# A graph layer's edge sums: the second half of each unit is summed first, and the first half is matched against 13 destinations instead of the second against 18

## The chip, the cores and the metric

The kernel runs on one core of one Trainium2 chip, as one launch. The metric is device microseconds of one execution, from the first to the last work of that core; lower is better. The five engines are named as the profile names them: PE (TensorE), DVE (VectorE), ACT (ScalarE), POOL (GpSimd) and SP (SyncE).

## The reference

The kernel computes one relational graph layer behind a layer norm, with N = 12,500 nodes, E = 212,500 edges, 256 features in and out and R = 8 edge types:

```python
src = concatenate([_s, _d, arange(12500)])     # 100,000 random pairs both ways, and a loop at every node
dst = concatenate([_d, _s, arange(12500)])
order = argsort(dst, stable=True)              # edges sorted by destination, a node's loop last
edge_type_8 = randint(0, 8, (212500,))

h = maximum(layernorm(x), 0)
hx = einsum('ni,rio->rno', h, weight)
agg = segment_sum(hx[edge_type, src], dst)
out = x + agg * 0.5**0.5 + h_bias + (h @ loop_weight) * 0.5**0.5
```

There are 17 edges to a destination on average (212,500 / 12,500), its own loop among them, and they come sorted by destination.

## The kernel before

**Sums first, weights after.** The kernel does not build `hx`. It sums the source rows of `h` for each pair of destination and type, and multiplies the sums by the eight weight matrices afterwards. `acc` in SBUF is a ring of 768 destinations by 8 types, transposed, in two chunks of 128 features (`KC` = 2).

**Units and tiles.** Edges are cut into units, and one unit fills at most two tiles of 128 edges (`PAIR` = 2). The first 128 units (block 0) have exactly 256 edges. Every later unit takes `EDGES` = 267 consecutive edges; the last edges of up to 22 destinations in it (the loops) are taken out and handled elsewhere (`last_edges`), and the others are moved together (`compacted`), so that the rest fits in 256 places. The very last unit takes what remains: 212,500 − 128·256 − 673·267 = 41 edges. So there are 802 units and, since the last has one tile only, 1,603 tiles. Blocks are groups of 128 units whose indices are prepared together, one unit per partition.

**A unit's window.** `bases` gives each unit a base destination: the destination of its first edge, held between bounds (`low`, `high`) that are worked out from the unit's number. Both bounds are themselves held between 0 and N − `WIN` = 12,478, so that a window of `WIN` = 22 destinations never leaves the graph. `columns` turns an edge into a column number (destination − base)·8 + type + 1, with 0 for an edge that falls outside of what its half is matched against. `REACH` gives that for each half as (first destination, number of destinations): in the kernel before, the first half of a unit reaches over destinations 0 to 21 of the window and the second over 4 to 21.

```python
def to():
    for h, _, n in halves:
        nc.vector.scalar_tensor_tensor(
            got["there"][:, h], got["col"][:, h], float(n * R), got["there"][:, h],
            op0=ALU.is_le, op1=ALU.mult)
```

`final`, `valid`, `sum_` and `all_` then set the columns outside to 0, count per unit the edges with a column above 0, add the loops that were taken out, and leave the number in `counts`.

**The check at the end, and the second way through.** When the last block is prepared, `verdict` adds all `counts` and compares the total with E:

```python
nc.vector.tensor_scalar(flag, pt[0:1, 0:1], float(E), None, op0=ALU.not_equal)
...
with tc.If(state["general"]):
    general_path(tc, x, src, dst, etype, bias, out, h32, w, wl, ident)
```

All engines load `flag` (`load`, L629) and branch on it at the end of the program (L1243), when all the work above is done. `general_path` computes the layer again for any edges at all, and it overwrites `out`. It is two loops at run time. `nodes` (97 rounds of 128 nodes and one of 84) loads 128 rows of `h32` and `x`, transposes the former, multiplies by the loop weights and then by each of the 8 weight matrices with one PSUM tile between PE and DVE, and stores 128 KB to `acc` and 1 MB to `hx` in DRAM. `edges` (1,660 rounds of 128 edges and one of 20) loads 128 sources, destinations and types one to a partition and the destinations once more as a 128x128 tile; compares them on DVE; gathers 128 rows of `hx` with an indirect DMA on POOL; multiplies by the 128x128 matrix of equal destinations on PE; copies the sums out on DVE; and adds them to `acc` with a second indirect DMA on POOL that accumulates in DRAM. Its pools have one buffer each, and between two rounds all engines meet. Last, `acc` is copied to `out`.

**The main loop.** For each tile, in an order written out by hand: `gather(t + 58)` issues the tile's 128 source rows as an indirect DMA on POOL (L755) into one of 60 buffers; every 48th tile is fetched row by row from SP instead (L767), with source numbers that `kept_sources` keeps. `onehots` compares four tiles' columns with a row of 1 to 176 on DVE (L785), which gives one-hots of 176 columns. `edge_sums` (L818) multiplies the gathered rows, as the stationary operand, with the one-hots: per tile two matmuls, one for each chunk of features, and each shows as two records in the trace. The first tile of a unit starts the PSUM bank and writes all 176 columns; the second adds its 18·8 = 144 columns from column 32 on. `add_sums` (L832) adds the bank to the ring on DVE. When a group of 128 destinations is complete, `product` (L1009) multiplies its sums by the weights, in pieces that are queued between the tiles. The gathers of the first 96 tiles read `x` and are normalised on ACT (L713), since `h32` isn't written yet.

Of the kernel before, what the change touches and what calls it, by code (L numbers as in the profile page):

```python
# [14 lines left out]
ALU = mybir.AluOpType  # L15
# [7 lines left out]
P = 128  # L23
# [9 lines left out]


WIN = 22
REACH = ((0, 22), (4, 18))

GROUP = 128

# [5 lines left out]
AHEAD = 58  # L45

SINGLE = 48
# [7 lines left out]
PAIR = 2  # L55
# [164 lines left out]
def kernel(  # L220
# [11 lines left out]
    nc = tc.nc  # L232
    N, D = x.shape
    E = src.shape[0]
    R = weight.shape[0]
    KC = D // P
    C = R * max(n for _, n in REACH)
    assert KC * R * WIN <= 512
    plan = Plan(N, E)

    NT = plan.NT
    U = PAIR * P
# [32 lines left out]

    def place_of(t):
        u, i = divmod(t, PAIR)
        return u // P, i, u % P


    with ExitStack() as main:
# [29 lines left out]
        msg, oh, offsets, kind = {}, {}, {}, {}  # L311
        firsts, stops, loops, marked, typed, gidx, col = {}, {}, {}, {}, {}, {}, {}
        added, zeroed = {}, {}
        single, fetches = {}, []
# [42 lines left out]
        def kept_sources(b, got):  # L357

            def keep():
                single[b] = idx.tile([P, P], I32, name="single")  # L360
                nc.vector.tensor_single_scalar(
                    single[b], got["sf"][:, P:U], float(D * 4), op=ALU.mult)

            return [keep]

# [115 lines left out]
        def columns(b, got):  # L481


            halves = [(slice(i * P, (i + 1) * P), o, n) for i, (o, n) in enumerate(REACH)]

# [18 lines left out]
                        got["there"][:, h], got["col"][:, h], float(o), None, op0=ALU.is_ge)  # L504

            def plain_to():
                nc.vector.scalar_tensor_tensor(
                    got["there"][:, :U], got["col"][:, :U], float(WIN), got["there"][:, :U],
                    op0=ALU.is_lt, op1=ALU.mult)

            def plain_typed():
                nc.vector.scalar_tensor_tensor(
# [67 lines left out]
            if b == 0:  # L580
                return [
                    bases, plain, plain_from, plain_to, plain_typed, plain_final, plain_sum, *turned(
                        got, "col", lambda: col.setdefault(b, cols.tile([P, U], F32, name="cols")))]
# [155 lines left out]
        def gather(t):  # L739
            if t % PAIR == 0:  # L740
                both = msgs.tile([P, PAIR, D], F32, name="msg")
                for i in range(PAIR):
                    msg[t + i] = both[:, i, :]
            if t % QUAD:
                kind[t] = kind[t - 1]
            else:
                kind[t] = "h" if state["h32"] is not None and t >= state["h32"] + LATE else "x"
            table = {"h": h32, "x": x}[kind[t]]
            b, i, u = place_of(t)
            if b and i and kind[t] == "h" and t % SINGLE == SINGLE - 1 and t + AHEAD < NT:  # L750
                for r in range(0, P, SOURCES):
                    fetches.append((done["tile"] + HOLD, lambda r=r: load_sources(t, r)))
                return
            at = i * P + u
            nc.gpsimd.indirect_dma_start(  # L755
                out=msg[t], out_offset=None, in_=table[:, :],
                in_offset=bass.IndirectOffsetOnAxis(ap=gidx[b][:, at : at + 1], axis=0))

        def load_sources(t, r0):

            b, _, u = place_of(t)
            _, vals = nc.values_load_multi_w_load_instructions(  # L762
                single[b][u : u + 1, r0 : r0 + SOURCES], engines=[SP],
                min_val=0, max_val=(N - 1) * D * 4,
                skip_runtime_bounds_check_because="clamped to the table where they are computed")
            for i, v in reversed(list(enumerate(vals))):
                fetches.insert(0, (0, lambda i=i, v=v: nc.sync.dma_start(  # L767
                    msg[t][r0 + i : r0 + i + 1, :].bitcast(U8),
                    h32_bytes[:, bass.ds(v, D * 4)])))
# [6 lines left out]
        def onehots(t):  # L776

            n = min(QUAD, NT - t)
            o = ohs.tile([P, QUAD // PAIR, PAIR, C], F32, tag="oh", name="oh")
            b, _, u = place_of(t)  # L780
            k = 0
            for v, i in ((n // PAIR, PAIR), (1, n % PAIR)):
                if v and i:
                    of = col[b].rearrange("p (i u) -> p u i", i=PAIR)[:, u + k : u + k + v, :i]
                    j = nc.vector.tensor_tensor(  # L785
                        o[:, k : k + v, :i, :],
                        iota_f.unsqueeze(1).unsqueeze(1).to_broadcast([P, v, i, C]),
                        of.unsqueeze(3).to_broadcast([P, v, i, C]), op=ALU.is_equal)
                    k += v
            for i in range(n):  # L790
                oh[t + i] = o[:, i // PAIR, i % PAIR, :]
                made[t + i] = j.ins.name

        def load_offsets(u0):
# [8 lines left out]
        def edge_sums(t):  # L803
            m, o = msg.pop(t), oh.pop(t)
            if t % PAIR == 0:
                bank = banks[t // PAIR % BANKS]
                sums["ps"] = bank[:, : KC * R * WIN].rearrange("p (c k) -> p c k", c=KC)
            ps = sums["ps"]
            i = t % PAIR
            from_, width = (a * R for a in REACH[i])  # L810
            end = t == NT - 1 or i == PAIR - 1
            free = added.get(t // PAIR - BANKS)
            if i == 0 and free is not None and latest["pe"] is not None:
                tc.add_manual_dep(latest["pe"], free.name, SYNC_DEP, reason="bank is free")
            if i == 0 and latest["pe"] is not None:
                tc.add_manual_dep(latest["pe"], made[t], SYNC_DEP, reason="one-hots are made")
            for c in range(KC):
                j = nc.tensor.matmul(  # L818
                    ps[:, c, from_ : from_ + width], m[:, c * P : (c + 1) * P], o[:, :width],
                    start=(i == 0 and c == 0), stop=(end and c == KC - 1))  # L820
            latest["pe"] = j.ins
            return ps
# [126 lines left out]
        got = {}  # L949
# [104 lines left out]
        with tc.manual_schedule():  # L1054
# [21 lines left out]
            for t in range(min(AHEAD, NT)):  # L1076
                gather(t)
# [76 lines left out]
            for t in range(0, min(NT, LEAD + 1), QUAD):  # L1154
                onehots(t)
            for t in range(NT):
                done["tile"] = t
                if t + AHEAD < NT:
                    gather(t + AHEAD)
# [22 lines left out]
                if t % QUAD == 2 and t + LEAD + QUAD - 2 < NT:  # L1182
                    onehots(t + LEAD + QUAD - 2)
                    credit -= 0.89
                if t % (PAIR * REGS) == 0 and t // PAIR + REGS < NU:
                    load_offsets(t // PAIR + REGS)
                ps = edge_sums(t)
                while late and late[0][0] <= t:
                    late.pop(0)[1]()
# [18 lines left out]
                while queue and (budget > 0 and t >= queue[0][0] or t >= queue[0][1]):  # L1208
                    _, _, c, f = queue.pop(0)
# [4 lines left out]
                while waiting and (len(waiting) > LAG or t == NT - 1):  # L1214
                    u, ps = waiting.pop(0)
# [54 lines left out]
```

## Time and profile before

| | |
|---|---|
| median of 3 runs | 2020.3 us (2017.76 to 2020.92) |
| profiled execution: its own time | 2023.05 us |
| its span from first to last instruction | 2021.3 us |
| mean granted TensorE clock | 0.957 |
| PE busy | 1796.2 us (89%) |
| POOL busy | 1500.7 us (74%) |
| DVE busy | 1317.4 us (65%) |
| ACT busy | 218.4 us (11%) |

The busy times are of one profiled execution. The share of POOL counts an indirect DMA's instruction (951 ns on average) and not the time between two of them. PE's time is a sum over pipelined matmuls, so a busy PE may still have room. Where rows carry a "q" behind the engine's name (SPq, POOLq, DVEq), they are of the engine's sequencer: DMA issues, semaphores, branches.

### The profile page before, as it was taken

The numbers are of one execution on the slowest core, as the hardware profiler recorded it, in microseconds if no ns is written. First come the engines' busy times: TensorE is split into PE (matmuls) and PEld (weight loads), VectorE is DVE, ScalarE is ACT, GpSimd is POOL, SyncE is SP. The second block draws the span as 40 slices with busy tenths as digits, with TensorE's granted clock in tenths as the row PEclk, the third lists the DMA queues.
The fourth block names the chain that finished last, engine by engine and source line by source line (L and its number), as shares of the span: only waits on it lengthen the run. The fifth ranks groups of instructions, "written<-read, shape, count | busy, mean of one in ns | idle before, by whom it ended". The sixth has DMA issues, their size and how long they took to land.

```text
span 2021.3 us, 36386 instructions
## 1 busy us (share of the span) xinstructions
PE 1796.2 (89%) x10411; PEld 1610.0 (80%) x10411; DVE 1317.4 (65%) x3281; ACT 218.4 (11%) x470; POOL 1500.7 (74%) x1602
## 2 busy tenths in 40 slices
PE   2468999997999898999899999998998898998998
PEld 2357999997888888988788788787787787787886
DVE  7869566687656578656577655577665568665642
ACT  7854110000000000000000000000000000000000
POOL 7766777777777777777777777777777777777773
PEclk8569999998999999999999999999999999999999
DMA  8973443444444444444444444444444444444442
GB/s 296 380 222 97 146 138 106 128 138 127 129 139 118 139 137 117 130 118 139 130 126 139 128 124 135 132 122 140 129 118 138 125 123 129 118 138 123 118 120 73
DMA packets 152577, 281.63 MB, mean 139 GB/s; under 512 B 31149, under 2 KB 101940, under 8 KB 152372
## 3 DMA queue, kind: packets, MB, share of 16 engines
q0 software_dynamic: 75648, 206.67, 35.1%
q1 hardware_dynamic: 76724, 72.61, 11.4%
q8 instruction: 82, 1.34, 0.3%
q14 instruction: 123, 1.01, 0.2%
HBM read 253.55 MB, written 25.60 MB: 138 GB/s over the span
## 4 chain that ended last, share of the span: by engine, by line
PE 38%; DMA 20%; SPq 17%; issue 12%; POOL 7%; DVE 5%; ACT 2%; DVEq 0%; POOLq 0%; ACTq 0%
PE ps L818 20%; PE po L1009 17%; DMA msg<-h,gidx 13%; SPq L767 13%; POOL msg L755 7%; SPq L762 4%; DMA hr<-h 2%; DMA h<-xt 1%; DVE e_stats L701 1%; DVE acc L832 1%; ACT xt L713 1%; DMA xr<-in_x_dram 1%; DMA w<-in_L_gnn_weight_dram 1%; DMA msg<-h 1%; DVE oh L785 1%
## 5 line engine op out<-in xcount | busy, mean ns | idle before, releaser
L755 POOL DMA_INDIRECT msg<-h,gidx x1480 | 1407.7, 951 | 464.2 <-issue 371.1
L818 PE MATMUL ps<-oh,msg 128*128 128x176 f32 (+1 forms) x6412 | 1169.6, 312 | 201.5 <-DMA msg<-h,gidx 78.5
L818 PEld LDWEIGHTS ps<-oh,msg 128*128 128x128 f32 x6412 | 1037.8, 196 | 355.3 <-DMA msg<-h,gidx 159.1
L1009 PE MATMUL po<-w,acc 128*128 128x256 f32 x3136 | 883.0, 383 | 1.8 <-DVE acc L832 1.8
L832 DVE TENSOR_TENSOR acc<-acc,ps 128x352 f32 x802 | 415.1, 518 | 503.4 <-PE ps L818 499.1
L1009 PEld LDWEIGHTS po<-w,acc 128*128 128x128 f32 x3136 | 537.6, 192 | 25.3 <-DVE acc L832 2.6
L785 DVE TENSOR_TENSOR oh<-fixed,cols 128x704 f32<-128x704 f32 x402 | 353.0, 879 | 0.0
L881 DVE SCALAR_TENSOR_TENSOR acc<-types,pt 128x256 f32<-128x256 bf16 (+1 forms) x688 | 249.0, 411 | 77.5 <-PE pt L859 71.5
L864 ACT ACTIVATE self_t<-pt 128x256 f32<-128x256 f32 x98 | 37.5, 383 | 1456.4 <-DVE acc L881 1352.5
L755 POOL DMA_INDIRECT msg<-in_x_dram,gidx x96 | 91.0, 948 | 31.1 <-issue 24.4
L1009 PE MATMUL po<-wl,self_t 128*128 128x256 f32 x392 | 105.2, 391 | 4.9 <-ACT self_t L864 2.5
L1009 PEld LDWEIGHTS po<-wl,self_t 128*128 128x128 f32 x392 | 69.1, 196 | 11.4 <-ACT self_t L864 2.9
L1021 DVE TENSOR_TENSOR xr<-xr,po 128x256 f32<-128x256 f32 x98 | 40.5, 413 | 17.5 <-PE po L1009 15.7
L713 ACT ACTIVATE xt<-xt,n_shift,n_rstd 128x256 f32<-128x256 f32 x98 | 50.9, 588 | 8.6 <-DVE n_shift L710 8.6
L713 ACT ACTIVATE msg<-msg,e_shift,e_rstd 128x256 f32<-128x256 f32 x96 | 49.6, 589 | 12.8 <-DVE e_shift L710 12.8
L1022 DVE TENSOR_TENSOR xr<-xr,po 128x256 f32<-128x256 f32 x98 | 41.2, 420 | 3.4
L934 ACT ACTIVATE diagonal<-ident,kinds 128x128 bf16<-128x128 f32 x88 | 28.1, 390 | 135.0 <-DVE kinds L931 130.1
L859 PE MATMUL pt<-ident,hr 128*128 128x128 f32 x196 | 37.9, 275 | 0.0
L370 DVE TENSOR_SCALAR moves<-fixed 128x267 int32<-128x267 int32 x84 | 36.0, 428 | 1.1
L701 DVE BATCH_NORM_STATS2 n_stats<-xt 128x6 f32<-128x256 f32 x98 | 34.4, 412 | 2.5 <-DMA xt<-in_x_dram 1.7
L371 DVE COPY_PREDICATED fixed<-moves,fixed 128x266 int32<-128x266 int32 (+6 forms) x84 | 33.7, 401 | 2.9
L701 DVE BATCH_NORM_STATS2 e_stats<-msg 128x6 f32<-128x256 f32 x96 | 33.5, 411 | 0.0
(201 smaller groups left out, 319.7 us busy)
## 6 DMA issues: line engine op xcount, KB each, us to landing
msg<-h SPq DMA_DIRECT2D x3456, 1.0 KB
msg<-h,gidx POOLq DMA_INDIRECT x1480
xt<-in_x_dram SPq DMA_DIRECT2D x24, 512.0 KB
h<-xt SPq DMA_DIRECT2D x24, 512.0 KB
xr<-in_x_dram SPq DMA_DIRECT2D x24, 512.0 KB
hr<-h SPq DMA_DIRECT2D x24, 512.0 KB
out_dram<-xr SPq DMA_DIRECT2D x24, 512.0 KB
w<-in_L_gnn_weight_dram SPq DMA_DIRECT2D x2, 1024.0 KB
```

The source lines that it names most:

```text
L701: nc.vector.bn_stats(stats[:n, j, :], rows_[j])
L713: nc.scalar.activation(rows_[j], rows_[j], AF.Relu, bias=shift[:n, j : j + 1], scale=rstd[:n, j : j + 1])
L755: nc.gpsimd.indirect_dma_start(out=msg[t], out_offset=None, in_=table[:, :], in_offset=bass.IndirectOffsetOnAxis(ap=gidx[b][:, at : at + 1 ...
L762: _, vals = nc.values_load_multi_w_load_instructions(single[b][u : u + 1, r0 : r0 + SOURCES], engines=[SP], min_val=0, max_val=(N - 1) * D ...
L767: fetches.insert(0, (0, lambda i=i, v=v: nc.sync.dma_start(msg[t][r0 + i : r0 + i + 1, :].bitcast(U8), h32_bytes[:, bass.ds(v, D * 4)])))
L785: j = nc.vector.tensor_tensor(o[:, k : k + v, :i, :], iota_f.unsqueeze(1).unsqueeze(1).to_broadcast([P, v, i, C]), of.unsqueeze(3).to_broa ...
L818: j = nc.tensor.matmul(ps[:, c, from_ : from_ + width], m[:, c * P : (c + 1) * P], o[:, :width], start=(i == 0 and c == 0), stop=(end and ...
L832: i = nc.vector.tensor_tensor(a, a, ps, op=ALU.add)
L881: i = nc.vector.scalar_tensor_tensor(acc[:, :, r, s0 : s0 + n], of, float(r + 1), pst[:, :, :n], op0=ALU.is_equal, op1=ALU.mult)
L1009: i = nc.tensor.matmul(got["out", g][:n], lhs, rhs, start=(r == R and c == 0), stop=(r == R - 1 and c == KC - 1))
L1021: nc.vector.tensor_add(rows_[:n, k, :], rows_[:n, k, :], outs[g % 2][:n, 1, :])
L1022: nc.vector.tensor_add(rows_[:n, k, :], rows_[:n, k, :], got["out", g][:n])
```

## The change

The two tiles of a unit change places in the order of the sums. `place_of(t)` gives a unit's even tile the second half of its edges and its odd tile the first half; the last unit, which has one tile, keeps its first half. The even tile starts the bank and writes 176 columns as before. The odd tile, now the first half, adds 13·8 = 104 columns from column 0 on. `REACH` is (0, 13) for the first half and (0, 22) for the second, and `columns` uses these numbers for all units. `kept_sources` keeps the first half's sources, as the tiles that SP fetches are odd. In block 0, `plain_to` becomes one instruction per half. The number and the order of all other instructions are the same; behind `plain_to` the lines of the kernel after stand two further down (L755 becomes L757, L818 becomes L820).

```diff
-REACH = ((0, 22), (4, 18))
+REACH = ((0, 13), (0, 22))
...
     def place_of(t):
         u, i = divmod(t, PAIR)
-        return u // P, i, u % P
+        half = 0 if PAIR * u + 1 == NT else PAIR - 1 - i
+        return u // P, half, u % P
...
                 single[b] = idx.tile([P, P], I32, name="single")
                 nc.vector.tensor_single_scalar(
-                    single[b], got["sf"][:, P:U], float(D * 4), op=ALU.mult)
+                    single[b], got["sf"][:, :P], float(D * 4), op=ALU.mult)
...
             def plain_to():
-                nc.vector.scalar_tensor_tensor(
-                    got["there"][:, :U], got["col"][:, :U], float(WIN), got["there"][:, :U],
-                    op0=ALU.is_lt, op1=ALU.mult)
+                for h, o, n in halves:
+                    nc.vector.scalar_tensor_tensor(
+                        got["there"][:, h], got["col"][:, h], float(o + n), got["there"][:, h],
+                        op0=ALU.is_lt, op1=ALU.mult)
...
-            if b and i and kind[t] == "h" and t % SINGLE == SINGLE - 1 and t + AHEAD < NT:
+            if b and t % PAIR and kind[t] == "h" and t % SINGLE == SINGLE - 1 and t + AHEAD < NT:
...
-                oh[t + i] = o[:, i // PAIR, i % PAIR, :]
+                oh[t + i] = o[:, i // PAIR, place_of(t + i)[1], :]
...
-            from_, width = (a * R for a in REACH[i])
+            width = R * (REACH[0][1] if i else WIN)
...
-                    ps[:, c, from_ : from_ + width], m[:, c * P : (c + 1) * P], o[:, :width],
+                    ps[:, c, :width], m[:, c * P : (c + 1) * P], o[:, :width],
```

## The prediction

> **What bounds the kernel now.** I read the page's groups first, then POOL's own instructions in order of time, the matmuls by shape, and the chain.
>
> ```profile
> L755 POOL DMA_INDIRECT msg<-h,gidx x1480 | 1407.7, 951 | 464.2 <-issue 371.1
> ```
>
> ```profile
> 127.55 0.95 POOL L755 DMA_INDIRECT msg<-h,gidx  x1 [0.30 <-issue]
> ...
> 133.88 0.94 POOL L755 DMA_INDIRECT msg<-h,gidx  x1 [4.14 <-ACT e_rstd L705]
> ...
> 140.96 0.95 POOL L755 DMA_INDIRECT msg<-h,gidx  x1 [4.89 <-issue]
> ...
> 1994.17 0.95 POOL L755 DMA_INDIRECT msg<-h,gidx  x1 [0.30 <-issue]
> 1995.42 1.17 POOL L755 DMA_INDIRECT msg<-h,gidx  x1 [0.30 <-issue]
> ```
>
> The second fence is POOL in order of time. A gather takes 0.95 us and the next comes 0.30 us later, 1.25 us in all, from 4.75 us to 1995.4 us. 1,575 steps of 1.25 us are 1,970 of these 1,991 us. The only longer gaps are six between 128 and 196 us, 14.7 us in sum. So the stream of gathers is the bound, not PE with its 89%.
>
> ```profile
> L818 PE MATMUL ps<-oh,msg 128*128 128x176 f32 x3208 | 645.8, 325 | 69.8 <-DMA msg<-h,gidx 37.4 <-ACT msg L713 29.5
> L818 PE MATMUL ps<-oh,msg 128*128 128x144 f32 x3204 | 562.2, 298 | 131.7 <-DMA msg<-h 45.5 <-DVE acc L832 43.7 <-DMA msg<-h,gidx 41.1
> ```
>
> In the matmuls by shape, PE itself waits for messages. A narrower matmul lets it wait longer.
>
> **What the change does as written.** Half of the matmuls go from 144 to 104 columns. In the chain below, four records of 176 columns take 0.60 us and four of 144 take 0.49, so 32 columns are worth 27 ns a record and 40 columns 34 ns: 3,204 records × 34 ns = 110 us of PE time. If the time to load 128 weight columns sets a floor, the nearest row is the transposes of 128 columns, 0.11 us apart, against 0.1225: 3,204 × 12 ns = 40 us. Either is off the bound. POOL issues as many gathers at the same pitch. The six early gaps are the only place where PE's pace could help, as POOL waits there for buffers that PE frees; but PE itself waited 10.1 us for ACT's normalising at 120 to 131 us. I bound this gain by 0 and 13 us (14.7 less six ordinary pitches' 0.30) and take 2. The other edits cost nothing that ends last: one more DVE instruction in block 0 (0.3 us at most, behind gathers that run anyway), the swapped halves (as many rows, the same 1 KB), the SP-fetched tiles (still odd, their sources from the half that is now odd). If only this counted, the time would be some 2,018 us.
>
> **The step that I think decides: the last unit.** `columns` takes 13 destinations for the first half of every unit. The last unit's base isn't its first destination: `high` holds it at 12,500 − 22 = 12,478. Its 41 edges belong, at 17 to a destination, to the last two or three nodes; I worked the reference's inputs through, and its first destination is 12,498, so its columns stand at destinations 20 and 21 of the window. Before, 22 reach them. Now `to` asks for a column of at most 13·8 = 104, and theirs are 161 and up: 39 edges (41 less two loops) are set to 0 and not counted. `edge_sums` does give this tile 176 columns, but the numbers are gone by then. In the other 801 units both halves fit. The total is 212,461, not 212,500, `flag` is 1, and all engines take the branch into `general_path`. It comes after everything else, so it is added whole.
>
> ```profile
> L629 DVEq TENSOR_LOAD <-flag x1: 311/311/311, 1772.6 to 1772.6; - x1
> ```
>
> ```profile
> L1243 POOLq INC_SWDGE_SEM  x1: 2016/2016/2016, 1993.3 to 1993.3; - x1
> ...
> L1243 DVEq COMPARE_BRANCH  x1: 72/72/72, 2016.9 to 2016.9; - x1
> ```
>
> The flag is read at 1773 us and DVE branches at 2017 us; nothing of the second way runs in the trace before, so its rounds are priced by near rows.
>
> ```profile
> 0.82 2.06 DMA nat_s<-in_src_dram
> ...
> 113.42 13.67 DMA w<-in_L_gnn_weight_dram
> ...
> 1979.16 2.73 DMA msg<-h,gidx
> 1984.17 4.06 DMA msg<-h,gidx
> ```
>
> ```profile
> 1994.16 0.49 PE ps L818 x4
> ...
> 1995.09 0.60 PE ps L818 x4
> ```
>
> ```profile
> L1266 SPq EVENT_SEMAPHORE  x14: 17/28/28, 2019.7 to 2021.3; - x14
> ...
> L1266 SPq DRAIN  x3: 7/7/13, 2020.5 to 2020.8; - x3
> ```
>
> The first of these is the chain of the whole run (start, duration), the second the chain near its end, the third the program's end.
>
> **A round of `edges`** is a string of waits, with one buffer each:
> - Loads: SP issues the third load 0.93 us after the first (0.82 and 1.75 us in its queue), and such a load lands 2.06 us later: 3.0 us. Columns of 4 bytes have no row; I allow 2.6 to 4.0.
> - DVE makes the row numbers from the third load: 0.14 and 0.16 us (128x1 rows) and a hand-over of 0.15: 0.45. Its other comparisons lie under the gather.
> - Gather: 2.73 to 4.1 us from POOL's start to landing; 2.8, since nothing else uses the queue.
> - PE, two records of 256 columns: 0.6 us at full clock, 1.2 at half (the profile grants 0.50 at 50 to 100 us, where PE is half idle); 1.0.
> - DVE copies the sums: 0.42 and two hand-overs: 0.6.
> - The accumulating scatter: no row. At least a gather's 2.75, and twice that, 5.5, if it reads and then writes; 4.0, between the two, since the fixed part needn't be paid twice.
> - The meeting of all engines: the program's end takes 0.8 us from SP's first drain to the last semaphore; twelve more semaphores are 0.3 us, the branch 0.07 to 0.23, and `INC_SWDGE_SEM` 0.03 us at the start of the program but 2.0 at its end. 1.2 to 3.3; I take 3.0, as its gathers are as fresh as at the end.
>
> Sum 14.85 us, between 10.95 and 19.2. Times 1,661: **24.7 ms**, between 18.2 and 31.8.
>
> The Trainium skill (DMA: Bandwidth & Descriptors, Anatomy of one DMA) puts one DMA at 2.0 us and bytes / 436 GB/s, 2.3 us for these 128 KB. The trace's gathers are dearer, 2.73 us at best. By the page's figure for gather and scatter the round would be 12.6 us by my estimate and the whole time 26.4 ms.
>
> **A round of `nodes`**: loads 2.5 (0.45 more than one), transposes 0.55, copy 0.6, loop weights 1.0 (four records of 256, 1.03 in PE's order of time); then eight times four records, a copy and two hand-overs (1.03 + 0.42 + 0.3 = 1.75, 14 in all; 22 at half clock), 16; the 1 MB store, 10 (the 1 MB of weights took 13.7 in a crowded stretch, 512 KB of `hr` 4.5 to 6.9); the meeting 3.0. Sum 33.7, between 29 and 45. Times 98: 3.3 ms, between 2.8 and 4.4. The last copy moves 12.8 MB both ways: 25.6 MB at the 380 GB/s of the busiest slice are 67 us, at the mean 139 GB/s 184; 0.1 ms.
>
> **Sum.** The profiled execution's own time is 2,023 us (span 2,021), 2.8 us above the median of the three runs, which doesn't matter here. 2.02 + 24.67 + 3.30 + 0.10 = **30.1 ms**. Ends: 23.1 and 38.4 ms.
>
> **Rivals.**
> - The second way is not taken (0.04). I would have to have misread the count; against that, the same reckoning of the kernel before gives 212,500 exactly. Then the stream of gathers decides, as above: 2,018 us, from 2,007 (all of the early gaps) to 2,023. Hence 0.01 for faster by more than 0.2% (about what a measurement of this kernel can tell from no change) and 0.03 for within 0.2%.
> - A dear round (0.10): the round costs 6 us more than my sum, in the accumulating scatter or in the branch back. From 20.9 us a round on, the whole is over 40 ms. For it speaks that neither has a row, and that the crowded queue's loads at 118 to 126 us took 2.1 to 2.8 us to issue alone; against it that the queue is empty here. The Trainium skill (Runtime: NRT & Kernel Launch, Instruction fetch mechanics) says that a taken branch to a target outside of the loaded instructions waits for a fetch; no run here shows its price, and a round has few instructions to an engine.
> - A cheap round (0.06): under 10.9 us, where columns of 4 bytes land as fast as one row and the meeting is 1 us: below 23 ms.
>
> That leaves 0.80 for 23 to 39 ms, with 30.1 the likeliest. All but the first rival are slower: 0.96.
>
> **What would show it.** Right: a span of tens of milliseconds; POOL's gathers of `msg` at 1.25 us to about 1,995 us as before, L820 with 3,204 records of 104 columns; then gathers of `g_m` and scatters to `gacc`, 1,661 each, at about 15 us, and PE nearly idle. The round's terms can be read one by one: the scatter's landing, the meeting, the loads. Wrong: no instruction of `general_path`, a total that still meets E, and a span near 2,020 us. If the span is right but `nodes` holds more than 5 ms or the round is far from 15 us, a term was mis-sized and the mechanism stands.

## The result, and the profile after

The changed kernel takes 27,117 us (median of 4 runs, 27,103 to 27,139) where the kernel before takes 2,019.5 (4 runs, 2,017.8 to 2,020.9): a ratio of 13.43, 95% interval 13.41 to 13.45. The profiled execution took 27,103.36 us, its span is 27,101.6. The forecast was 30,100, between 23,000 and 39,000.

The head of the page and its costliest groups now belong to other lines:

```profile
span 27101.6 us, 191436 instructions
...
L203 PE MATMUL g_ps<-g_m,g_same 128*128 128x256 f32 x3322 | 1979.1, 699 | 20385.2 <-DMA g_m<-hx,g_of 19575.5
L199 POOL DMA_INDIRECT g_m<-hx,g_of x1661 | 1643.6, 990 | 14341.2 <-DVE g_of L196 11653.7
L206 POOL DMA_INDIRECT gacc<-g_ss,g_to x1661 | 2629.8, 1583 | 6427.3 <-DVE g_ss L205 6427.3
```

L199, L203 and L206 are `edges` in `general_path`, which did not run at all before. Each of the 1,661 gathers and scatters is there (PE's 3,322 records are two a round), and PE idles 20,385 us in front of its own. The branch, in DVE's sequencer:

```profile
L1245 DVEq COMPARE_BRANCH  x2: 55/58/61, 2015.6 to 27055.6; - x2
```

Before, DVE met its branch once, at 2016.9 us. Now the first branch on this line is at 2015.6 us and the second is 25 ms later, where the branch's block ends. The first way itself is as long as it was. The end of it, in order of time:

```profile
1993.18 0.95 POOL L757 DMA_INDIRECT msg<-h,gidx  x1 [0.30 <-issue]
1994.43 0.96 POOL L757 DMA_INDIRECT msg<-h,gidx  x1 [0.30 <-issue]
```

The last gather starts at 1994.43 us (before: 1995.42), still at a pitch of 1.25 us, and DVE's last instruction of the first way ends at 2016.0 us (before: 2017.3). Each of these is read from one execution, and the kernel before alone spreads from 2,017.8 to 2,023.05 us, so 1.0 and 1.3 us are no difference that needs a cause.

One round of `edges` from the middle, in order of time:

```profile
15009.22 0.34 SPq L178 DMA_DIRECT2D g_s<-in_src_dram  x1
...
15012.20 0.15 DVE L180 CAST g_tf<-g_t 128x1 f32<-128x1 int32 x1
...
15012.81 0.99 POOL L199 DMA_INDIRECT g_m<-hx,g_of  x1 [7.03 <-DVE g_of L196]
...
15015.68 0.50 PEld L203 LDWEIGHTS g_ps<-g_m,g_same 128*128 128x128 f32 x2 [12.95 <-DVE g_to L194]
...
15016.95 0.42 DVE L205 COPY g_ss<-g_ps 128x256 f32<-128x256 f32 x1 [1.38 <-PE g_ps L203]
15017.65 1.58 POOL L206 DMA_INDIRECT gacc<-g_ss,g_to  x1 [3.85 <-DVE g_ss L205]
15022.65 0.34 SPq L178 DMA_DIRECT2D g_s<-in_src_dram  x1
```

The starts can be subtracted one from the next: loads 2.98 us, row numbers 0.61, gather 2.87, matmul 1.27, copy and hand-over 0.70, scatter and meeting 5.00; 13.43 in all. From the first round's load at 4,693.0 us to the last's at 27,049.3 the mean round is 13.47 us. The sequencers split the last 5.00 us (rows of the loop's line, L212, here of the three meetings between 15,000 and 15,040 us):

```profile
L212 SPq DRAIN  x9: 7/7/7, 15008.2 to 15035.7; - x9
...
L212 POOLq INC_SWDGE_SEM  x3: 218/218/218, 15008.5 to 15035.4; - x3
```

The scatter in the round before began at 15,004.20 us, SP's first drain is at 15,008.2 and the next load at 15,009.22: 4.0 us for the scatter to land, 1.0 for the meeting of all engines.

### The profile page after: what moved, and what is told of

Read it like the earlier page. It is cut to its first block, busy times and chain, and to the rows that moved or that the text cites. A ratio compares the mean times of both kernels' runs of the same rounds, so it can differ in the third digit from the quotient of the medians.

```text
span 27101.6 us, 191436 instructions
## 1 busy us (share of the span) xinstructions
PE 5262.3 (19%) x17457; PEld 3309.1 (12%) x17457; DVE 6151.7 (23%) x24292; ACT 218.6 (1%) x470; POOL 5772.2 (21%) x4927
## 3 DMA queue, kind: packets, MB, share of 16 engines
q0 software_dynamic: 394448, 642.08, 12.6%
## 5 line engine op out<-in xcount | busy, mean ns | idle before, releaser
L203 PE MATMUL g_ps<-g_m,g_same 128*128 128x256 f32 x3322 | 1979.1, 699 | 20385.2 <-DMA g_m<-hx,g_of 19575.5
L199 POOL DMA_INDIRECT g_m<-hx,g_of x1661 | 1643.6, 990 | 14341.2 <-DVE g_of L196 11653.7
L206 POOL DMA_INDIRECT gacc<-g_ss,g_to x1661 | 2629.8, 1583 | 6427.3 <-DVE g_ss L205 6427.3
L203 PEld LDWEIGHTS g_ps<-g_m,g_same 128*128 128x128 f32 x3322 | 830.7, 310 | 21533.0 <-DVE g_to L194 21340.4
L757 POOL DMA_INDIRECT msg<-h,gidx x1480 | 1405.1, 949 | 465.4 <-issue 366.2
L205 DVE COPY g_ss<-g_ps 128x256 f32<-128x256 f32 x1661 | 705.5, 425 | 2791.4 <-PE g_ps L203 2791.4
L166 PE MATMUL g_pr<-w,g_ht 128*128 128x256 f32 x3136 | 1261.2, 542 | 354.5 <-DVE g_hs L169 354.5
L820 PE MATMUL ps<-oh,msg 128*128 128x176 f32 (+1 forms) x6412 | 1124.2, 304 | 221.6 <-DMA msg<-h,gidx 92.6
L820 PEld LDWEIGHTS ps<-oh,msg 128*128 128x128 f32 x6412 | 1018.0, 197 | 386.8 <-DMA msg<-h,gidx 188.7
L166 PEld LDWEIGHTS g_pr<-w,g_ht 128*128 128x128 f32 x3136 | 757.7, 263 | 853.9 <-DVE g_hs L169 740.3
L187 DVE TENSOR_TENSOR g_earlier<-g_same,before 128x128 f32<-128x128 f32 x1661 | 486.0, 293 | 57.6
L185 DVE TENSOR_SCALAR g_same<-g_same,g_df 128x128 f32<-128x128 f32 x1661 | 475.2, 286 | 58.9
L189 DVE TENSOR_REDUCE g_moved<-g_earlier 128x1 f32<-128x128 f32 x1661 | 474.9, 286 | 56.6
```

The costliest lines, as they stand in the source:

```text
L166: nc.tensor.matmul(pr[:n], ht[:, c, :n], w[:, c, r * D : (r + 1) * D], start=(c == 0), stop=(c == KC - 1))
L185: nc.vector.tensor_scalar(same[:n, :n], same[:n, :n], c["d"][:n], None, op0=ALU.is_equal)
L187: nc.vector.tensor_mul(earlier[:n, :n], same[:n, :n], before[:n, :n])
L189: nc.vector.tensor_reduce(moved[:n], earlier[:n, :n], AX.X, ALU.max)
L199: nc.gpsimd.indirect_dma_start(out=m[:n], out_offset=None, in_=hx[:, :], in_offset=bass.IndirectOffsetOnAxis(ap=of[:n, 0:1], axis=0))
L203: nc.tensor.matmul(ps[:n], same[:n, :n], m[:n], start=True, stop=True)
```

## Experiments

The chips that ran the kernel are of two kinds. In the first runs, and on the chip of the run without SP rows, the kernel before takes 2,020 us (the first kind); on the four other chips it takes 2,560 to 2,590 (the second kind). So a time is compared only with the kernel before on the same chip. Each of those four was used on one occasion, so it is not shown that the chip itself makes the difference.

**Only the count is mended.** A per-unit limit in the last block, 13 destinations for all and 22 for the last unit.

```diff
+limit = 13 * R + (tid[:, NB - 1] >= NU - 1) * (WIN - 13) * R        # one number to a partition
...
-    got["there"][:, h], got["col"][:, h], float(n * R), got["there"][:, h],
+    got["there"][:, h], got["col"][:, h], limit if b == NB - 1 and i == 0 else float(n * R), ...
```

> The changed kernel, with one thing more: in the last block the first half's limit is held per unit, 13 destinations for all and 22 for the last unit (two small DVE instructions at the start make it). Theory, the last unit's 39 uncounted edges alone send the program into the second way: it isn't taken, and what is left is the first way of the changed kernel, whose last DVE instruction ended at 2016.0 us against 2017.3 before: about 2018.5 us, a ratio of 0.9994, within 0.2% of before. Rival, other first halves overrun 13 destinations too, or the swapped order loses edges: still 27.1 ms.

2,593.5 us against 2,591.5 of the kernel before: a ratio of 1.0009 (0.9983 to 1.0036). It was run twice more, on other chips:

> The kernel of the first run again, for its ratio to the kernel before, on whatever chip this call gets. Theory: within 0.2% of before, as the flag stays 0 and POOL or SP sets the time, not PE: 0.9994 on a chip like the first. Rival, PE's saving shows where nothing else is in the way: under 0.99.

1.0001 (0.9974 to 1.0028).

> The kernel of the first run once more, as the last call got a chip on which the kernel before takes 2021 us again. Theory, POOL's gathers set the time there: 0.9994 of before, 2019.5 us, within 0.2%. Rival, PE's 30 to 50 us come through: 0.975 to 0.985, 1970 to 1990 us.

0.9985 (0.9966 to 1.0004), on a chip where before takes 2,565.7 us, not the kind that was hoped for. `general_path` doesn't run in any of the three: the branch row of the first has one execution, not two.

```profile
L1250 DVEq COMPARE_BRANCH  x1: 72/72/72, 2570.5 to 2570.5; - x1
```

So the 39 uncounted edges are all that opens the second way in the changed kernel. And what is left of the change is worth nothing that these runs can measure. The three runs say this of the second kind of chip only. There POOL's stream isn't all that counts: in the first of the three POOL waits 225 us for PE, and its last gather starts at 2,492.2 us, 83 us before the end (26 us in the trace before). For the first kind there is the first way of the changed kernel, which ends at 2,016.0 us, and the run without SP rows below.

**Only the count is broken.** The kernel before, order and widths untouched, with the same limit turned round (22 for all, 13 for the last unit).

> The kernel before, order and widths unchanged; only the last unit's first half is matched against 13 destinations and not 22. Its 39 edges are left out of the first way's sums and of the count. Theory: all of the loss follows from these edges, so the time is that of the changed kernel within the noise, 27,100 to 27,140 us, with the first way ending at 2017.3 us as before. Rival, the swapped halves or the narrower one-hots have a part in it: 2020 us, or clearly under 27.1 ms.

27,729.8 us (one run) where the kernel before takes 2,591.5 on that chip: 25,138 us more. The changed kernel has 27,117 − 2,019.5 = 25,098 us more. The absolute time was expected without the slower first way; the difference agrees within 0.2%. One unit of 41 edges in 212,500 makes the whole loss, and the swap and the narrower one-hots have no part in it.

**Only the order is swapped.** `REACH = ((0, 22), (0, 22))`: odd tiles add 176 columns.

> The changed order, but the first half too is matched against 22 destinations: odd tiles add 176 columns, not 104, and not 144 as before. The last unit is counted. PE has 3204 x 27 ns = 88 us more to do than before. Theory, the stream of gathers on POOL sets the time: the same as before within 0.2%, 2019 to 2024 us, POOL's pitch 1.25 us to the end, PE waiting less for messages; what there is beyond that comes from the early stretch (128 to 196 us), where POOL waits for buffers. Rival, PE sets the time: up to 2105 us.

> The swapped order with 22 destinations for both halves (176 columns in the odd tiles, 88 us more of PE's time than before) once more, for a chip like the first. Theory, POOL's gathers set the time: 2020 to 2026 us, at most 0.3% over before. Rival, PE sets the time: up to 2105 us.

1.0028 (1.0006 to 1.0049) and, on another chip, 1.0009 (0.9985 to 1.0032). The second way doesn't run, so the swap loses no edges. 88 us more of PE's work cost 7 us by the first run's middle value, which is a little over the 0.2% expected, and 13 us by the end of its interval; the rival's 85 us are excluded on these chips. Neither is of the first kind, so these runs don't test POOL's stream as the bound.

**Odd tiles of 72 columns.** The first experiment with `width = R * 9` for odd tiles.

> As the first kernel, with the odd tiles' matmuls at 72 columns; the sums of each first half's destinations 9 to 12 are left out, the count isn't. Theory, a floor from loading 128 weight columns: four records of 72 columns follow each other as those of 104 do, 0.42 to 0.43 us, where 144 columns took 0.49. Rival, the width alone: 32 columns less are 0.11 us less, 0.32 us. The time as in the first kernel either way, 2018.5 us, as POOL's gathers set it.

2,589.4 us (one run), before 2,591.5. PE in order of time, first the kernel before, then the changed kernel, then this one:

```profile
708.16 0.65 PE L818 MATMUL ps<-oh,msg 128*128 128x144 f32 x4
708.65 1.03 PE L1009 MATMUL po<-w,acc 128*128 128x256 f32 x4
709.51 0.76 PE L818 MATMUL ps<-oh,msg 128*128 128x176 f32 x4
```

```profile
701.80 0.59 PE L820 MATMUL ps<-oh,msg 128*128 128x104 f32 x4
702.22 1.05 PE L1011 MATMUL po<-w,acc 128*128 128x256 f32 x4
703.11 2.23 PE L820 MATMUL ps<-oh,msg 128*128 128x176 f32 x16
```

```profile
1100.88 0.56 PE L822 MATMUL ps<-oh,msg 128*128 128x72 f32 x4
1101.28 0.64 PE L1013 MATMUL po<-w,acc 128*128 128x256 f32 x2
1101.76 0.76 PE L822 MATMUL ps<-oh,msg 128*128 128x176 f32 x4
```

From start to next start, four records take 0.49 us at 144 columns, 0.42 at 104 and 0.40 at 72, at a granted clock of 1.00 in all three places. The width alone would give 0.11 us for the last 32 columns; 0.02 came. The starts of single records in the traces show where it stops: of the four steps one follows the width (0.09 us at 104 columns, 0.06 at 72), and the other three take 0.11 us at both widths. So there is a floor of 0.11 us a record, the price at which the transposes stood in the prediction; that the loading of the weights makes it is not shown. The four products that follow take 0.89 us behind 104 columns and 0.86 behind 144, so of the 17 ns that a record saves some 7 are given back. From 104 to 72 all is given back: four records and the two products behind them take 0.88 us at 72 columns (1,100.88 to 1,101.76) and 0.88 at 104 on the same chip (709.94 to 710.82 us of the first run with the count mended).

**Fewer rows from SP, with and without the change.** Every 64th tile instead of every 48th comes from SP.

```diff
-SINGLE = 48
+SINGLE = 64
```

> The kernel of the first run (the change with the last unit counted), with every 64th tile and not every 48th fetched row by row from SP (20 of them for 27): POOL gathers 7 tiles more, 7 x 1.25 = 9 us. In the runs so far on chips where the kernel before takes 2560 to 2590 us, SP's rows followed each other in 0.59 us (0.45 where it takes 2020), and PE waited for them. Theory, SP's queue is the bound on such a chip: 128 rows in 64 tiles' time are 75 us under 80, so the bound goes back to POOL's gathers, and the time is 2030 to 2060 us there, and 2027 us on a chip like the first. Rival, something else is slow on such a chip: still above 2500 us.

> The kernel before, with every 64th tile fetched from SP. Against the run with the same number and the change, it says what the narrower odd tiles are worth. Theory, nothing that can be measured where POOL's gathers set the time: the two within 0.2% of each other (2 us in favour of the change at most 13). Rival, PE's 30 to 50 us come through in full: the change 1.5 to 2.5% faster.

2,506.2 us with the change (0.9697 of the kernel before, 0.9666 to 0.9728) and 2,508.0 without (0.9714, 0.9679 to 0.9748). The two don't differ. Both beat the kernel before on this chip of the second kind by 3%, which is not the change's doing, and the theory of 2,030 to 2,060 us fell: SP's queue is not what makes these chips slower, or not alone.

**No rows from SP.** `SINGLE = 4000`, with the last unit counted.

> The kernel of the first run (the change with the last unit counted), with no tile fetched row by row from SP: POOL gathers all 1,603 tiles, 27 more, 27 x 1.25 = 34 us. On a chip like the first the stream of gathers then gives 2052 us. On chips where the kernel before takes 2560 to 2590 us: theory, the rows from SP are what is slow there and hold up the rest: 2050 to 2150 us, under the kernel before by 17% or more. Rival, PE, DVE and POOL stall there whether or not SP fetches (stretches of some 3 us in which PE issues one record in 0.71 us): 2450 us or more.

This run was on a chip of the first kind: before 2,021.0 us, this 2,052.7, a ratio of 1.0159 (1.0142 to 1.0176). So the question about the second kind of chip stays unanswered, but another was answered, as the first sentence expected 2,052: 27 more gathers at 1.25 us are 34 us, and 32 came. The end of POOL's stream:

```profile
2026.08 0.94 POOL L759 DMA_INDIRECT msg<-h,gidx  x1 [0.30 <-issue]
2027.33 0.95 POOL L759 DMA_INDIRECT msg<-h,gidx  x1 [0.31 <-issue]
```

The last gather starts at 2,027.3 us, 32 us later than before. PE had the narrower tiles here and waited 143.7 us for gathers (before: 78.5). So on this kind of chip POOL's stream sets the first way's time.

**Two rounds between meetings.** `general_path` takes two rounds of `edges` in one loop body, with two buffers for each tile.

```diff
-with tc.For_i(0, total // P * P, P) as i:
-    body(i, P)
+with tc.For_i(0, total // (2 * P) * 2 * P, 2 * P) as i:        # edges only
+    body(i, P)
+    body(i + P, P)
```

> The changed kernel; in the second way the loop over edges takes two rounds of 128 edges between two meetings of all engines, with two buffers of each tile (830 rounds of 256 edges and the last 20). Theory, a round is a string of waits (loads 3.3 us, gather 2.9, matmul and copy 1.9, scatter to landing 4.0, meeting 1.0), so two strings overlap but for the scatters, of which the second waits for the first to land: some 18.5 us for two, 830 x 18.5 = 15.4 ms, and 2.0 + 2.7 + 15.4 = 20.1 ms in all. Rival, the engines' and queues' own time fills the round, so only the meeting is saved: 2 x 12.4 + 1.0 = 25.9 us for two, 26.2 ms in all.

20,247.6 us (one run; the kernel before on that chip: 2,562.6). Two rounds take 18.98 us on the mean, (20,193.0 − 4,441.8) / 830, where 18.5 was expected and 25.9 by the rival.

```profile
15008.52 1.61 POOL L206 DMA_INDIRECT gacc<-g_ss,g_to  x1 [1.25 <-DVE g_ss L205]
...
15013.17 1.58 POOL L206 DMA_INDIRECT gacc<-g_ss,g_to  x1 [3.04 <-DMA gacc<-g_ss,g_to]
15018.51 0.34 SPq L178 DMA_DIRECT2D g_s<-in_src_dram  x1
```

The second scatter waits 3.04 us for the first to land. The second round adds 5.5 us to the 13.47 of one; 4.65 of them lie between the starts of the two scatters, so all else of the second round but some 0.9 us lies beside the first. The total came out as expected with two parts off that cancel: the first way is 0.5 ms longer on this chip, and the second buffers shorten a round of `nodes` from 27.4 to 19.3 us, 0.8 ms in all.

**A scatter that does not add.** `compute_op=ALU.add` taken out of the scatter.

> The changed kernel; the scatter to the accumulator overwrites its rows and doesn't add (the additions in DRAM are left out). In the changed kernel POOL's instruction for it took 1.58 us and the landing 4.0 us from its start. Theory, adding makes it read the row first: without it POOL's instruction is 0.99 us as a gather's, the landing 2.9 us, the round 1.1 us shorter, 25.3 ms in all. Rival, landing in DRAM is what takes long: the round within 0.6 us of 13.4, 26.1 to 27.1 ms.

25,355 us (one run), of which 22,793 are above the kernel before on that chip, 2,305 us less than the changed kernel's 25,098. A round is 12.09 us, 1.38 shorter.

```profile
15012.28 0.99 POOL L206 DMA_INDIRECT gacc<-g_ss,g_to  x1 [3.86 <-DVE g_ss L205]
15015.90 0.34 SPq L178 DMA_DIRECT2D g_s<-in_src_dram  x1
```

From the scatter's start to the next load 3.62 us instead of 5.00, and POOL's instruction 0.99 instead of 1.58. Adding costs 1.4 us of the round, slightly more than the 1.1 expected.

## Why the prediction was right, and where it was off

- **The last unit's edges are not counted, and the branch is taken.** Right, and shown from both sides: mending the count alone brings the time back, breaking it alone brings the loss.
- **The second way comes whole behind the first.** Right: it starts at 2,015.6 us and adds 25.1 ms.
- **What bounds the first way, and what the rest of the change is worth.** Right. That POOL's stream sets it on the first kind of chip is shown by the run without SP rows (32 us for 27 gathers). The forecast of 2,018 for this part compares with a first way that ends 1.3 us earlier than before, which is within what the kernel before spreads by itself. POOL's early gaps did not shrink (5.82 and 5.79 us for the two largest, before 4.14 and 4.89), so the 2 us that I took from them didn't come from there. Of the two prices for PE, 110 us and 40, the runs favour the lower: 17 ns a record, 10 after what is given back, are 32 to 54 us, all off the bound.
- **The sum.** Forecast 2.02 + 24.67 + 3.30 + 0.10 ms; the trace has 2.02 + 22.36 + 2.68 + 0.04. It was 3.0 ms too dear, within a wide range. The terms that were mis-sized:
  - The meeting of all engines: 3.0 us forecast, 1.0 measured. I took `INC_SWDGE_SEM` at the program's end (2.0 us) for its price; in the loop it is 0.218, and at the end of the run without SP rows 0.445, so 2.0 us is no fixed price. Over 1,661 rounds the meeting is 3.3 ms too much. The matmul, the hand-overs and the row numbers were 0.1 to 0.3 us dearer than forecast and gave 0.9 ms back. For the matmul the price at half clock was the right one: from 4,690 to 27,055 us the granted clock is 0.50, and the two records take 1.19 us (forecast 1.2 at half clock, 1.0 taken).
  - The 1 MB store in `nodes`: 10 us forecast, 4.2 measured (5.19 from its issue at 2,036.77 us to the next round's load, less a meeting's 1.0). The 13.7 us of the weights' load, in a crowded stretch, was no row for an idle queue. With the 2.0 us of the meeting this makes 7.8; the rest, PE above all, was dearer than forecast and gave 1.5 back. So a round of `nodes` takes 27.4 us on the mean, 6.3 less than the 33.7 and under the lower end of 29. No round takes the mean: 50 take 24 us and 47 take 31, by PE's clock (last section).
  - Landed as forecast: the loads (2.98 for 3.0), the gather (2.87 for 2.8), the scatter (4.0 for 4.0, by luck, as it was a guess between 2.75 and 5.5).
- **The Trainium skill's figure.** By the Trainium skill (DMA: Bandwidth & Descriptors, Anatomy of one DMA) a gather and a scatter of 128 KB would take 2.3 us each, an estimate from its 2.0 us and bytes / 436 GB/s. The trace has 2.87 and 4.0 us from the start of POOL's instruction, and the measurement decides. The round that I worked out with it, 12.6 us, is nearer to the measured 13.47 than my 14.85 only because my meeting was 2.0 us too dear in both.
- **The dear round.** It didn't come: there is 1.0 us from SP's first drain to the next load. The Trainium skill (Runtime: NRT & Kernel Launch, Instruction fetch mechanics) says that a taken branch to a target outside of the loaded instructions waits for a fetch. The trace shows no such wait in these short bodies. Each engine also has a `BRANCH_PREFETCH_HINT` of 31 to 39 ns in a round (L1268), so it is open whether the short body or the hint spares it.

The step of the last unit carried more than all the sums: a limit that suits 801 units of 802 is a limit that the program refuses for all.

## What to carry to other kernels

Before sizing what a tighter bound saves, try it on the element that sits at the clamp: the last unit, whose window is pushed back from the edge, uses the columns that the others leave empty. Where a kernel checks itself and falls back, the fall-back's price belongs to every change of a bound, as one row in 212,500 can call it. A round with single buffers costs the sum of its waits: price it row by row from an idle queue. A second buffer took away nearly all of a round here but the wait that must stay in order.

## What the runs showed of the hardware that was not expected

- The same kernel takes 2,020 us on the first kind of chip and 2,560 to 2,590 on the second, while a round of `edges` is the same on both (13.47 and 13.45 us): the second way adds 25,098 us on one and 25,138 on the other. On the second kind there are stretches in which PE issues one record in 0.71 us with nothing that the profile shows to wait for, here in the run of 72 columns, in order of time:

```profile
1105.17 0.22 PE L822 MATMUL ps<-oh,msg 128*128 128x72 f32 x1 [0.32 <-issue]
1105.89 0.32 PE L822 MATMUL ps<-oh,msg 128*128 128x72 f32 x1 [0.49 <-issue]
1106.60 0.22 PE L822 MATMUL ps<-oh,msg 128*128 128x72 f32 x1 [0.39 <-issue]
1107.32 0.47 PE L822 MATMUL ps<-oh,msg 128*128 128x72 f32 x1 [0.49 <-issue]
```

  In the same stretch DVE stands for 3.2 us and POOL for 1.9, and the profile puts both down to `remote`, a release whose source it doesn't show. In the first run with the count mended DVE's additions to the ring wait 356 us for `remote` and POOL's gathers 219; the traces of the first kind of chip have no such wait. Fewer SP rows take 3% off. What causes it stays open.
- A matmul record narrower than 104 columns gains nothing here: three of four steps take 0.11 us at 104 columns and at 72, and what the fourth gains the products behind it give back.
- PE's granted clock steps up and down in a loop whose rounds are all the same. In `nodes` a round takes 23.9 us seven times on end, then 30.9 to 31.0 us nine times on end, and so on. The first two of these stretches follow; behind the busy times of the five engines stand the granted clock (0.79 and 0.50), the DMA share and GB/s:

```profile
2042.00:2209.00 167.00, 84.06 (x266) 52.69 (x266) 32.68 (x77) 0.00 (x0) 0.00 (x0) 0.79 0.16 60
2212.00:2430.00 218.00, 133.72 (x269) 78.03 (x269) 33.09 (x78) 0.00 (x0) 0.00 (x0) 0.50 0.12 46
```

  Four records and their copy take 1.65 us in the first stretch and 2.59 in rounds of the long kind. In `edges`, where PE is busy for 9% of the time, the clock is 0.50 on the mean of the whole loop. What switches it is not shown.
- An accumulating scatter of 128 rows of 1 KB to DRAM costs 1.4 us more than one that overwrites, of which 0.6 are POOL's own.
